# A four-layer graph network on one core: the general path as one loop at the end, norms and neighbour weights in pieces, norm rows by small transfers, transposes beside a product

## The chip, the core and the metric

The kernel runs on one core of a Trainium2 chip. A core has five engines with a queue of instructions each: TensorE (PE; its weight loads are listed apart as PEld), VectorE (DVE), ScalarE (ACT), GpSimd (POOL) and SyncE (SP), which here only issues DMA transfers. GpSimd issues some transfers too. An engine works through its own queue in order; where an instruction needs another engine's result it waits, and all behind it in that queue waits as well. The metric is device microseconds of one execution. The kernel before takes 11451.39 us, the median of three runs (11443.48 to 11453.73).

## What is computed

There are N = 3327 nodes with D = 128 features and a dense matrix adj of zeros and ones, N by N. Four layers follow each other, each behind a layer norm with a relu, and each added to x:

```python
def reference(x, adj, ...):
    relu_norm = lambda x: jnp.maximum(_layernorm(x), 0.0)
    h = relu_norm(x)                                    # layer 0
    x1 = swish(adj @ h @ W + b)
    x = x + swish(adj @ x1 @ W + b)
    h = relu_norm(x)                                    # layer 1: 128 heads of 8
    a = softmax(q @ k.T * 128**-0.5 + adj + adj)        # per head, N x N
    x = x + (a @ v, all heads) @ Wo.T
    h = relu_norm(x)                                    # layer 2
    msg = relu(adj @ h @ W_msg.T + b_msg)
    x = x + gru_cell(msg, h)                            # r, z, n; three products each
    h = relu_norm(x)                                    # layer 3
    d = 1 / sqrt(adj.sum(-1))
    z = leaky_relu(d * (adj @ (d * h)) @ W1 + b1, 0.1)
    d2 = max(|z_i|^2 + |z_j|^2 - 2 z_i . z_j, 0)
    S = exp(-sqrt(d2 + 1e-10) / 2), kept for the 4 largest of a row
    A2 = S + adj;  e = 1 / sqrt(A2.sum(-1))
    return x + e * (A2 @ (e * h)) @ W2 + b2
```

## The kernel before

*Layout.* Nodes lie in T = 26 tiles of P = 128 partitions: partition p holds the rows p*26 + t, one for each tile t. x (`xs`), h and the like are arrays of 128 x 26 x 128 in fp32; a transposed array (`hT`, `zT`, `agg`) has the features on partitions and the nodes along the row. `quads()` gives tiles by fours (six of four and one of two); the norm works in three pieces of 4, 9 and 13 tiles (`CUTS`).

*Order.* The instructions of each engine stand in the order of the program, with a planner that moves them a little within a stage; waits come from the use of tiles and of their memory. A memory pool (`tc.tile_pool`) gives its memory back at its end, and the next pool that takes it waits for the last use. Layer 0 and the attention of layer 1 (an order written out by hand) end at 10565.82 us and are not touched. Everything after them is, and it is called the tail here. In the order of time:

- *Projection* (lines 650 to 669). For each tile SyncE loads o (128 x 9 x 128) from the scratch tensor `ot`; VectorE takes the reciprocal of the sums (658) and multiplies (659); TensorE transposes eight times (664), ScalarE copies (665), TensorE multiplies with Wo (668), and VectorE adds the result to xs (669).
- *Norm of layer 2* (`layernorm_relu`, 146 to 153), after all 26 tiles, in three pieces, each followed by `split` (202 to 205): half of h as a sum of three bf16 arrays, `parts`.
- *Product 2* (`adj_matmul_parts`, 214 to 217): 26 tiles of `adj16`, twice the adjacency in bf16, are loaded (a16, four buffers) and each multiplied with three parts in seven column blocks. `evacuate` copies the seven accumulators to `agg` (177, 179). Behind every such product stands a loop `For_i(0, n_once)` (227) with an fp32 product. `n_once` is read once from a flag that the kernel computes, at line 554, and is 0 for these inputs: the loop is passed without a turn. A further such loop (557) stands between the attention and the projection, with a general attention in it.
- *Gates* (684 to 707): h is transposed to hT (`transposed`, 240 to 244), then per 512 nodes the message, the gates and yT; yT is transposed back and added to xs (711, 712).
- *Norm of layer 3*, times d1 (723), split, and *product 3*.
- *z and squares* (734 to 769): z per quad, leaky relu over all rows (738), transposes to zT, z squared and its sums nsq, z2T = 2 zT; then per 512 nodes zT squared (757), its sum over the features by a matmul (759), and three bf16 rows of it in `n_rows`, on partitions 0, 32 and 64 (765 to 769).
- *Top four* (782 to 788): per tile of 128 nodes TensorE makes 2 z.z of it with all nodes and adds the norm rows (782, 785), ScalarE adds nsq and writes `dist` (786), VectorE finds the eight largest and their indices (MAX8 787, FIND_INDEX8 788).
- *Weights* (791 to 804), after all tiles: near, sim, deg2, d2, y = h*d2 with its split, y stored to `yd` in memory (803), b2 added to xs.
- *Product 4 with gathers* (815 to 830): after the loads of each tile of the product, `beside(t)` lets GpSimd gather the four neighbours' rows of yd by indirect DMA (815), VectorE weigh and add them to a tile g (822, 824), and, LAG = 10 tiles later, TensorE transpose g (829). g has LAG + 2 = 12 buffers. Then the empty loop, the last transposes, the product with W2 (846, 847), scaling (849), the sum with xs (850) and the stores (853).

Of the kernel before, what the change touches and what calls it, by code (L numbers as in the profile page):

```python
# [8 lines left out]
F32 = mybir.dt.float32  # L9
# [11 lines left out]
P = 128  # L21
# [32 lines left out]
def kernel(  # L54
# [79 lines left out]
    def pieces():  # L134
        return [(slice(t0, t1), t1 - t0) for t0, t1 in zip(CUTS, CUTS[1:]) if t1 > t0]

    def layernorm_relu(pool, then=None, tmp=None):
# [7 lines left out]
        for p, n in pieces():  # L145
            nc.vector.tensor_reduce(mean[:, p], xs[:, p], AX.X, ALU.add)
            nc.vector.tensor_scalar_mul(mean[:, p], mean[:, p], 1.0 / D)
            nc.vector.tensor_sub(xc[:, p], xs[:, p], over_t(mean, p.start, n))
            nc.scalar.activation(sq[:, p], xc[:, p], AF.Square)
            nc.vector.tensor_reduce(var[:, p], sq[:, p], AX.X, ALU.add)  # L150
            nc.scalar.activation(rstd[:, p], var[:, p], AF.Sqrt, bias=eps_c, scale=1.0 / D)
            nc.vector.reciprocal(rstd[:, p], rstd[:, p])
            nc.vector.scalar_tensor_tensor(h[:, p], xc[:, p], 0.0, over_t(rstd, p.start, n), op0=ALU.max, op1=ALU.mult)  # L153
            if then is not None:
                then(h, p, n)
        return h
# [42 lines left out]
    def split(pool, parts, y, p, n):  # L199

        rest = pool.tile([P, T, D], F32, name="rest")
        nc.scalar.activation(parts[0][:, p], y[:, p], AF.Copy, scale=0.5)
        nc.vector.scalar_tensor_tensor(rest[:, p], y[:, p], 0.5, parts[0][:, p], op0=ALU.mult, op1=ALU.subtract)
        nc.scalar.copy(parts[1][:, p], rest[:, p])
        nc.vector.tensor_sub(parts[2][:, p], rest[:, p], parts[1][:, p])

    def adj_matmul_parts(agg, parts, lhs, n_once, on_tile=None):
# [19 lines left out]
        with tc.For_i(0, n_once, 1):  # L227
            adj_matmul(agg, lhs, bufs=1)
# [18 lines left out]


# [14 lines left out]
    with tc.tile_pool(name="l0", bufs=1) as pool:  # L263
        h = layernorm_relu(pool)
# [47 lines left out]
        nc.vector.tensor_add(deg[:, T - 1 : T], deg[:, T - 1 : T], fix)  # L312

# [49 lines left out]
    with tc.tile_pool(name="l1", bufs=1) as pool, tc.tile_pool(name="l1_ps", bufs=3, space=PSUM) as ps:  # L363
# [9 lines left out]
        with tc.tile_pool(name="l1_ln", bufs=1) as ln, tc.tile_pool(name="l1_tp", bufs=2, space=PSUM) as tps:  # L373
            hT = transposed(pool, tps, layernorm_relu(ln), "hT")
# [177 lines left out]


# [78 lines left out]

    weights = ctx.enter_context(tc.tile_pool(name="weights", bufs=1))
    w1_s = load_w(w1, [D, D], "w1_s")
    w2_s = load_w(w2, [D, D], "w2_s")
    w_msg_s = load_w(w_msg, [D, D], "w_msg_s")
    w_ih_s = load_w(w_ih, [D, 3, D], "w_ih_s")
    w_hh_s = load_w(w_hh, [D, 3, D], "w_hh_s")
    b_msg_s = load_w(b_msg, [D, 1], "b_msg_s")
    b_ih_s = load_w(b_ih, [D, 3], "b_ih_s")  # L640
    b_hh_s = load_w(b_hh, [D, 3], "b_hh_s")
    b1_s = load_w(dram(b1, 0, [[0, P], [1, D]]), [P, D], "b1_s")
    b2_s = load_w(dram(b2, 0, [[0, P], [1, D]]), [P, D], "b2_s")
    b_rz = weights.tile([D, 3], F32, name="b_rz")
    nc.vector.tensor_add(b_rz, b_ih_s, b_hh_s)


    with tc.tile_pool(name="lo", bufs=3) as pool, tc.tile_pool(name="lo_ps", bufs=2, space=PSUM) as ps:
        wo_s = pool.tile([NH, E, D], F32, name="wo_s", bufs=1)
        nc.gpsimd.dma_start(wo_s, wo)  # L650
        for t in range(T):
            kp = rows_of(t)
            o = pool.tile([P, EA, NH], F32, name="o")
            src = ot.rearrange("e (p t c) -> t p e c", t=T, c=NH)[t]
            for p0, p1 in ((0, kp),) if kp == P else ((0, 112), (112, kp)):
                nc.sync.dma_start(o[p0:p1], src[p0:p1])
            inv = pool.tile([P, NH], F32, name="inv")
            nc.vector.reciprocal(inv[:kp], o[:kp, E, :])
            nc.vector.tensor_mul(o[:kp, :E, :], o[:kp, :E, :], inv[:kp].unsqueeze(1).to_broadcast([kp, E, NH]))
            oT = pool.tile([NH, E, P], F32, name="oT")  # L660
            for half in range(2):
                tp = ps.tile([P, 4, P], F32, name="tp")
                for j in range(4):
                    nc.tensor.transpose(tp[:, j, :kp], o[:kp, 4 * half + j, :], ident[:kp, :kp])
                nc.scalar.copy(oT[:, 4 * half : 4 * half + 4, :kp], tp[:, :, :kp])
            yp = ps.tile([P, D], F32, name="yp")
            for e in range(E):
                nc.tensor.matmul(yp[:kp], oT[:, e, :kp], wo_s[:, e, :], start=(e == 0), stop=(e == E - 1))
            nc.vector.tensor_add(xs[:kp, t, :], xs[:kp, t, :], yp[:kp])


    with tc.tile_pool(name="l2", bufs=1) as pool:
        parts = three_parts(pool)
        h = layernorm_relu(pool, lambda h, p, n: split(pool, parts, h, p, n))
        agg = new_agg(pool)
        adj_matmul_parts(agg, parts, h, n_once)
        with tc.tile_pool(name="l2_tp", bufs=2, space=PSUM) as tps:
            hT = transposed(pool, tps, h, "hT")
        yT = pool.tile([P, NP], F32, name="yT")
        with tc.tile_pool(name="l2_w", bufs=2) as wk2, tc.tile_pool(name="l2_ps", bufs=1, space=PSUM) as ps:  # L680
            for c0, w in chunks(NP, 512):
                hc = hT[:, c0 : c0 + w]
                mp = ps.tile([P, 512], F32, name="mp", bufs=2)
                nc.tensor.matmul(mp[:, :w], w_msg_s, agg[:, c0 : c0 + w], start=True, stop=True)
                msg = wk2.tile([P, 512], F32, name="msg")
                nc.scalar.activation(msg[:, :w], mp[:, :w], AF.Relu, bias=b_msg_s)
                gates = []
                for k in range(2):
                    gp = ps.tile([P, 512], F32, name=f"gp{k}")
                    nc.tensor.matmul(gp[:, :w], w_hh_s[:, k, :], hc, start=True, stop=False)  # L690
                    nc.tensor.matmul(gp[:, :w], w_ih_s[:, k, :], msg[:, :w], start=False, stop=True)
                    gate = wk2.tile([P, 512], F32, name=f"gate{k}")
                    nc.scalar.activation(gate[:, :w], gp[:, :w], AF.Sigmoid, bias=b_rz[:, k : k + 1])
                    gates.append(gate)
                r, z = gates
                hn = ps.tile([P, 512], F32, name="hn")
                nc.tensor.matmul(hn[:, :w], w_hh_s[:, 2, :], hc, start=True, stop=True)
                inn = ps.tile([P, 512], F32, name="inn")
                nc.tensor.matmul(inn[:, :w], w_ih_s[:, 2, :], msg[:, :w], start=True, stop=True)
                n = wk2.tile([P, 512], F32, name="n")  # L700
                nc.vector.scalar_tensor_tensor(n[:, :w], hn[:, :w], b_hh_s[:, 2:3], r[:, :w], op0=ALU.add, op1=ALU.mult)
                nc.vector.tensor_add(n[:, :w], n[:, :w], inn[:, :w])
                nc.scalar.activation(n[:, :w], n[:, :w], AF.Tanh, bias=b_ih_s[:, 2:3])
                y = yT[:, c0 : c0 + w]
                nc.vector.tensor_sub(y, hc, n[:, :w])
                nc.vector.tensor_mul(y, y, z[:, :w])
                nc.vector.tensor_add(y, y, n[:, :w])
            for t0, n in quads():
                tp = ps.tile([P, 4, P], F32, name="tp", bufs=2)
                for j in range(n):  # L710
                    nc.tensor.transpose(tp[:, j, :], slots(yT)[:, t0 + j, :], ident)
                nc.vector.tensor_add(xs[:, t0 : t0 + n, :], xs[:, t0 : t0 + n, :], tp[:, :n, :])


    yd = dpool.tile([NP, D], F32, name="yd")
    keep = ctx.enter_context(tc.tile_pool(name="l3_s", bufs=1))
    with tc.tile_pool(name="l3", bufs=1) as pool:
        d1 = inv_sqrt(keep, deg, "d1")
        y = keep.tile([P, T, D], F32, name="y")
        parts = three_parts(keep)  # L720

        def weighted(h, p, n):
            nc.vector.tensor_mul(y[:, p], h[:, p], over_t(d1, p.start, n))
            split(pool, parts, y, p, n)

        h = layernorm_relu(keep, weighted, pool)
        agg = new_agg(pool)
        adj_matmul_parts(agg, parts, y, n_once)
        z = pool.tile([P, T, D], F32, name="ln_xc")
        with tc.tile_pool(name="l3_ps", bufs=2, space=PSUM) as ps:  # L730
            for t0, n in quads():
                zp = ps.tile([P, 4, D], F32, name="zp")
                for j in range(n):
# [162 lines left out]
```

## Time and profile before

| | us |
|---|---|
| median of three runs | 11451.39 |
| profiled execution | 11471.65 |
| its span | 11469.9 |
| attention ends (last copy of o) | 10565.82 |
| first o tile in use; last sum with xs | 10584.39; 10674.16 |
| product 2: first matmul; first copy of its result | 10685.43; 10795.90 |
| first gate matmul | 10814.45 |
| product 3: first matmul; first copy | 10875.99; 10986.75 |
| first MAX8 | 11057.09 |
| last index found | 11245.71 |
| product 4: first matmul; first gather | 11251.25; 11260.56 |

The mean TensorE clock granted over the span is 0.985 of full speed. A row of a timeline gives the start in us, the busy time, the engine, the line, the operation with output and input, the number of instructions, and in brackets how long the engine had been idle before and what released it; "issue" means that the profile shows nothing that it waited for. SPq is SyncE's queue, where transfers are issued. A row of a group gives the count, the busy time with the mean in ns, and the idle time before it. In the rows of tenths the span is cut into 40 slices, 287 us each.

### The profile page before, as it was taken

The page shows a single profiled execution, that of the slowest core. Times are in us where ns is not written, and L with a number is a line of the kernel's source. Part 1 is how long each engine was busy: PE and PEld are TensorE (multiplying, and loading weights), DVE is VectorE, ACT ScalarE, POOL GpSimd, SP SyncE. Part 2 cuts the span into 40 slices and gives each one's busy share as a digit, 9 for nine tenths or more (in the row PEclk, how much of TensorE's full clock was granted, in tenths as well). Part 3 has the DMA queues.
Part 4 walks back from the last instruction along what each step waited for, and adds up shares of the span by engine and source line. Part 5 has one row for each costly group of instructions (what it writes and reads, how often), then busy time and mean ns, then how long its engine had stood idle before and what let it go on. Part 6 is the DMA issues. An engine that isn't in the chain of part 4 may idle for free. (4 is left out here: it accounts for less than half of the span.)

```text
span 11469.9 us, 212317 instructions
## 1 busy us (share of the span) xinstructions
PE 11060.2 (96%) x80114; PEld 3113.4 (27%) x80114; DVE 9433.5 (82%) x15530; ACT 10214.1 (89%) x9169; POOL 5699.5 (50%) x6205
## 2 busy tenths in 40 slices
PE   9789999999999999999999999999999999999887
PEld 4322222222222222222222222222222222222553
DVE  8578888888888888888888888888888888887464
ACT  0389999999999999999999999999999999998221
POOL 0145555555555555555555555555555555554003
PEclk9899999999999999999999999999999999999998
DMA  7854444343434444444444444434444434343313
GB/s 268 237 118 63 67 64 67 61 69 62 69 61 67 62 69 62 68 62 66 64 66 65 61 67 61 69 60 67 61 68 62 65 57 60 56 61 73 123 57 114
DMA packets 475718, 888.18 MB, mean 77 GB/s; under 512 B 91380, under 2 KB 422629, under 8 KB 439092
## 3 DMA queue, kind: packets, MB, share of 16 engines
q1 hardware_dynamic: 470226, 864.60, 42.6%
q8 instruction: 640, 10.49, 0.4%
q0 software_dynamic: 4448, 9.79, 0.3%
q14 instruction: 404, 3.31, 0.1%
HBM read 763.28 MB, written 110.74 MB: 76 GB/s over the span
## 5 line engine op out<-in xcount | busy, mean ns | idle before, releaser
L484 DVE TENSOR_TENSOR p<-early,a 128x476 f32<-128x476 f32 (+1 forms) x14560 | 8434.5, 644 | 1393.2 <-PE early L479 1160.2
L489 ACT ACTIVATE p<-p 128x2380 f32<-128x2380 f32 (+1 forms) x2912 | 6830.1, 2345 | 8.5
L496 PE MATMUL acc<-p,v 128*9 128x476 f32 (+1 forms) x46592 | 5847.5, 564 | 25.9 <-POOL p L487 7.1
L487 POOL TENSOR_TENSOR p<-p,e 128x476 f32<-128x476 f32 (+1 forms) x2912 | 3535.7, 1214 | 3317.7 <-ACT p L485 3271.5
L485 ACT ACTIVATE p<-late 128x476 f32<-128x476 f32 (+1 forms) x5824 | 4592.2, 923 | 32.3 <-DMA k_in<-kt 21.3
L479 PE MATMUL early<-q,k 32*128 32x476 f32 (+1 forms) x14560 | 2885.5, 477 | 19.9 <-DVE p L484 19.9
L479 PE MATMUL late<-q,k 32*128 32x476 f32 (+1 forms) x8736 | 2797.3, 478 | 64.3 <-ACT p L485 36.2
L360 POOL CAST k<-k_in 128x256 fp32r<-128x256 f32 x2912 | 1943.9, 701 | 1115.9 <-DMA q<-qt 579.2
L479 PEld LDWEIGHTS late<-q,k 32*128 32x128 f32 x8736 | 1065.4, 181 | 4775.4 <-ACT p L485 3318.4
L482 PE MATMUL late<-a,two_i 128*128 128x476 bf16 (+1 forms) x5824 | 2180.8, 374 | 0.0
L479 PEld LDWEIGHTS early<-q,k 32*128 32x128 f32 x14560 | 1147.3, 181 | 26.8 <-DVE p L484 20.6
L496 PEld LDWEIGHTS acc<-p,v 128*9 128x9 f32 x46592 | 709.0, 88 | 1367.8 <-issue 1184.9
L482 PEld LDWEIGHTS <-two_i 128*128 128x128 bf16 x5824 | 556.4, 96 | 1326.6 <-issue 1326.6
L217 PE MATMUL agg_ps<-a,part 128*128 128x512 bf16 (+1 forms) x1638 | 351.7, 375 | 91.7 <-issue 50.1
L177 ACT COPY agg<-agg_ps 128x512 f32<-128x512 f32 x15 | 8.2, 591 | 481.9 <-PE agg_ps L191 290.5
L815 POOL DMA_INDIRECT row<-yd,idx x104 | 99.6, 958 | 461.1 <-DMA yd<-y 393.7
L217 PEld LDWEIGHTS <-part 128*128 128x128 bf16 x1638 | 163.1, 100 | 276.2 <-issue 76.3
L260 POOL TENSOR_SCALAR a<-a_in 128x476 bf16<-128x476 f32 (+2 forms) x156 | 222.5, 1426 | 0.5
L786 ACT ACTIVATE dist<-sp,nsq 128x2048 f32<-128x2048 f32 (+1 forms) x52 | 85.6, 1647 | 114.3 <-PE sp L785 104.0
L394 ACT ACTIVATE qk_st<-pp 128x1024 fp32r<-128x1024 f32 (+1 forms) x52 | 53.2, 1023 | 147.8 <-DMA qt<-qk_st 61.3
L260 POOL TENSOR_SCALAR a<-a 128x476 bf16<-128x476 f32 (+1 forms) x26 | 36.4, 1399 | 295.8 <-DMA a<-in_adjT_dram 295.8
L191 PE MATMUL agg_ps<-a,h 128*128 128x512 f32 (+2 forms) x364 | 148.1, 570 | 24.0 <-DVE h L153 24.0
(186 smaller groups left out, 2602.0 us busy)
## 6 DMA issues: line engine op xcount, KB each, us to landing
k_in<-kt SPq DMA_DIRECT2D x1792, 208.0 KB
v<-vd SPq DMA_DIRECT2D x896, 117.0 KB
a<-in_adjT_dram SPq DMA_DIRECT2D x50, 1663.5 KB
a<-adj SPq DMA_DIRECT2D x78, 831.8 KB
q<-qt SPq DMA_DIRECT2D x3072, 14.9 KB
a_in<-in_adjT_dram SPq DMA_DIRECT2D x125, 238.0 KB
qt<-qk_st SPq DMA_DIRECT2D x25, 1024.0 KB
kt<-qk_st SPq DMA_DIRECT2D x25, 1024.0 KB
```

The source lines that it names most:

```text
L191: nc.tensor.matmul(acc[c][:, :w], lhs[:kp, t, :], a[:kp, c0 : c0 + w], start=(t == 0), stop=(t == T - 1))
L217: nc.tensor.matmul(acc[c][:, :w], part[:, t, :], a[:, c0 : c0 + w], start=(t == 0 and i == 0), stop=(t == T - 1 and i == 2),)
L260: nc.gpsimd.tensor_scalar(a2[:kp, :w], a, 2.0, None, op0=ALU.mult)
L360: nc.gpsimd.tensor_copy(k, slots(k_in)[:, t : t + 2, :])
L479: nc.tensor.matmul(sp[:, :we], pairs[t // 2][r, t % 2, :], q4[r, :we], start=True, stop=ways[i] != "I")
L482: nc.tensor.matmul(late[:, i - n_d, :we], two_i, a2[:, :we], start=False, stop=True)
L484: nc.vector.tensor_tensor(p8[:, places[i], :we], early[i][:, :we], a2[:, :we], op=ALU.add)
L485: nc.scalar.activation(p8[:, places[n_d] : places[3] + 1, :we], late[:, :, :we], AF.Exp)
L487: nc.gpsimd.tensor_tensor(p8[:, places[3], :we], p8[:, places[3], :we], e_a[:, :we], op=ALU.mult)
L489: nc.scalar.activation(p8[:, :5, :we], p8[:, :5, :we], AF.Exp)
L496: nc.tensor.matmul(acc[32 * i : 32 * i + EA, :w], v4[:kp, i, t, :], p8[:kp, PLACES[t % 2][i], :w], start=(t == 0), stop=(t == T - 1),)
L815: nc.gpsimd.indirect_dma_start(out=row, out_offset=None, in_=yd, in_offset=bass.IndirectOffsetOnAxis(ap=idx[:, t, k : k + 1], axis=0),)
```

## The change

- *The general path in one place.* The tail becomes a function `tail(general)`. It is called with False first; at the end of the kernel stands one loop `For_i(0, n_once)`, which holds the general attention, the reload of xs from a copy `x1d` that is stored after layer 0, and `tail(True)`. The loops behind the products and the one before the projection are gone, and the flag is read at the end.
- *Norms in pieces as rows come.* `layernorm_relu` returns h and a function `done(t)`; a piece is worked off as soon as its rows are added to xs: in the projection's loop, and in the loop over the quads that adds the GRU's result. `split` takes y already halved, as `halved` and `d1_half` make it.
- *Transposes beside product 2.* A quad of h is transposed at each odd tile of the product; the stage of transposes in front of the gates is gone.
- *z and squares by quads.* The leaky relu, z squared (on GpSimd now), its sums, zT and z2T (both straight from the transposes in PSUM, on ScalarE) come quad by quad. The norm rows are no longer summed by a matmul: nsq (128 x 26) is split into three bf16 arrays, each stored to a scratch row of `nd` by a small transfer, and one more transfer reads the three rows as `n_rows`, on three partitions.
- *Neighbour weights in pieces.* `second(p, n)` does lines 791 to 803 for a piece of tiles as soon as the top-four loop has passed it; y and its split are GpSimd's work for the first two pieces and VectorE's for the last; yd is stored in three pieces. The indices get a min with the last row. The sum with b2 goes to GpSimd, after product 3.
- *Buffers.* LAG is 6 and g has 8 buffers. The pools are merged to a single one for layers 2 and 3 (`l23`), whose arrays take each other's names and memory: `zT` that of hT, `z2T` that of yT, `gT` that of ln_sq. The pool `lo` lies inside it.

Lines that only move are left out of this diff:

```diff
-    def adj_matmul_parts(agg, parts, lhs, n_once, on_tile=None):
+    def adj_matmul_parts(agg, parts, on_tile=None):
...
             evacuate(agg, acc)
-        with tc.For_i(0, n_once, 1):
-            adj_matmul(agg, lhs, bufs=1)
...
+    def in_pieces(f):
+        todo = [slice(t0, t1) for t0, t1 in zip(CUTS, CUTS[1:]) if t1 > t0]
+        def done(t):
+            while todo and todo[0].stop <= t:
+                p = todo.pop(0)
+                f(p, p.stop - p.start)
+        return done
...
+        nc.gpsimd.dma_start(x1d, xs)
...
                 for t in range(T):
...
                     nc.vector.tensor_add(xs[:kp, t, :], xs[:kp, t, :], yp[:kp])
+                    done(t + 1)
...
+                def transpose_quad(t):
+                    if t % 2 and left:
+                        t0, n = left.pop(0)
+                        tp = tps.tile([P, 4, P], F32, name="tp")
+                        for j in range(n):
+                            nc.tensor.transpose(tp[:, j, :], h[:, t0 + j, :], ident)
+                        nc.vector.tensor_copy(slots(hT)[:, t0 : t0 + n, :], tp[:, :n, :])
+                adj_product(agg, y, parts, transpose_quad)
...
-            nc.vector.scalar_tensor_tensor(z, z, 0.1, z, op0=ALU.mult, op1=ALU.max)
-            zT = transposed(pool, ps, z, "zT")
-        nc.vector.tensor_mul(zz, z, z)
-        nc.vector.tensor_reduce(nsq, zz, AX.X, ALU.add, negate=True)
-        nc.scalar.activation(z2T, zT, AF.Copy, scale=2.0)
+                    nc.vector.scalar_tensor_tensor(z[:, q], z[:, q], 0.1, z[:, q], op0=ALU.mult, op1=ALU.max)
+                    for j in range(n):
+                        nc.tensor.transpose(tp[:, j, :], z[:, t0 + j, :], ident)
+                    nc.scalar.activation(slots(z2T)[:, q, :], tp[:, :n, :], AF.Copy, scale=2.0)
+                    nc.scalar.copy(slots(zT)[:, q, :], tp[:, :n, :])
+                    nc.gpsimd.tensor_mul(zz[:, q], z[:, q], z[:, q])
+                    nc.vector.tensor_reduce(nsq[:, q], zz[:, q], AX.X, ALU.add, negate=True)
-                nc.tensor.matmul(np_[:, :w], neg_ones[:, :PR], zzT[:, :w], start=True, stop=True)
...
+            for i in range(3):
+                nc.vector.tensor_copy(n3[:, i, :], src)
+                if i < 2:
+                    nc.vector.tensor_sub(rest[:, i, :], src, n3[:, i, :])
+                    src = rest[:, i, :]
+                nc.sync.dma_start(nd[i].rearrange("(p t) -> p t", t=T), n3[:, i, :])
+            nc.sync.dma_start(n_rows, nd)
...
+            def second(p, n):
+                nc.vector.tensor_scalar(idx[:, p, :4], idx[:, p, :4], NP - 1, None, op0=ALU.min)
+                nc.vector.tensor_scalar(near[:, p], top[:, p, :4], 0.0, None, op0=ALU.min)
+                nc.scalar.activation(sim[:, p], near[:, p], AF.Sqrt, bias=tiny_c, scale=-1.0)
+                nc.scalar.activation(sim[:, p], sim[:, p], AF.Exp, scale=-0.5)
...
+                engine = nc.gpsimd if p.stop < T else nc.vector
+                engine.tensor_mul(y[:, p], h[:, p], over_t(d2_half, p.start, n))
+                split_unless_general(pool, parts, y, p, engine)
+                nc.sync.dma_start(yd.rearrange("(p t) f -> p t f", t=T)[:, p], y[:, p])
...
                 nc.vector.max_index(idx[:, t, :], top[:, t, :], dist)
+                done(t + 1)
...
-        gs, LAG = [], 10
+            gs, LAG = [], 6
...
+    tail(False)
     n_once = nc.values_load(n_gen[0:1, 0:1], min_val=0, max_val=1)
     with tc.For_i(0, n_once, 1):
...
+        nc.sync.dma_start(xs, x1d)
+        tail(True)
```

## Prediction

> **What bounds the kernel now.** I read the page first, then the trace in the order of time.
>
> ```profile
> span 11469.9 us, 212317 instructions
> PE   9789999999999999999999999999999999999887
> L217 PE MATMUL agg_ps<-a,part 128*128 128x512 bf16 (+1 forms) x1638 | 351.7, 375 | 91.7 <-issue 50.1
> L815 POOL DMA_INDIRECT row<-yd,idx x104 | 99.6, 958 | 461.1 <-DMA yd<-y 393.7
> ```
>
> TensorE is busy in 96% of the span, but only the last three digits of its row, which drop to 8 and 7, are touched: up to the end of the attention (10565.8 us) all engines but POOL get the same instructions in the same order, and POOL has one more, the store of x1d. It stands ahead of three weight loads that are issued at 359 us and first used at 378.8; its 1.7 MB cost some 4.3 us at 400 GB/s, which that slack hides. So the prediction is about 904 us, 10566 to 11470. The timelines of TensorE, VectorE and SyncE cut them at the points where an engine waited:
>
> ```profile
> 10584.39 0.95 DVE L658 RECIPROCAL inv<-o 128x128 f32<-128x128 f32 x1 [17.92 <-DMA o<-ot]
> 10674.16 0.29 DVE L669 TENSOR_TENSOR xs<-xs,yp 127x128 f32<-127x128 f32 x1 [2.91 <-PE yp L668]
> 10685.43 24.78 PE L217 MATMUL agg_ps<-a,part 128*128 128x512 bf16 x113 [11.31 <-ACT part L202]
> 10795.90 2.21 DVE L179 COPY agg<-agg_ps 128x512 f32<-128x512 f32 x4 [95.36 <-PE agg_ps L217]
> 10814.45 1.10 PE L684 MATMUL mp<-agg,w_msg_s 128*128 128x512 f32 x2 [0.82 <-DVE hT L244]
> 10857.35 6.31 PE L711 MATMUL tp<-ident,yT 128*128 128x128 f32 x26 [3.37 <-DVE yT L707]
> 10875.99 34.36 PE L217 MATMUL agg_ps<-a,part 128*128 128x512 bf16 x159 [12.32 <-ACT part L202]
> 10986.75 2.21 DVE L179 COPY agg<-agg_ps 128x512 f32<-128x512 f32 x4 [88.98 <-PE agg_ps L217]
> 10993.42 12.02 PE L734 MATMUL zp<-w_s,agg 128*128 128x128 f32 x52 [5.52 <-issue]
> 11057.09 3.63 DVE L787 MAX8 top<-dist 128x8 f32<-128x3327 f32 x1 [8.52 <-ACT dist L786]
> 11245.71 0.19 DVE L791 TENSOR_SCALAR near<-top 128x104 f32<-128x104 f32 x1
> 11254.23 0.32 SPq L803 DMA_DIRECT2D yd<-y  x1
> 11260.56 1.10 POOL L815 DMA_INDIRECT row<-yd,idx  x1 [393.73 <-DMA yd<-y]
> 11285.75 0.38 PE L217 MATMUL agg_ps<-a,part 128*128 128x512 bf16 x1 [2.42 <-issue]
> 11339.63 10.65 PE L217 MATMUL agg_ps<-a,part 128*128 128x512 bf16 x40 [0.81 <-issue]
> 11357.36 0.94 POOL L815 DMA_INDIRECT row<-yd,idx  x1 [26.07 <-DVE g L822]
> 11440.34 0.47 PE L829 MATMUL tp<-ident,g 128*128 128x128 f32 x1 [5.21 <-issue]
> ```
>
> Two stretches, of the squares and of the last product, in the view by windows (us, then busy time and instructions of PE, PEld, DVE, ACT, POOL, then PEclk, DMA share, GB/s):
>
> ```profile
> 11000.00:11050.00 50.00, 26.52 (x70) 13.77 (x70) 40.81 (x66) 10.37 (x11) 0.00 (x0) 0.64 0.00 0
> 11300.00:11350.00 50.00, 19.63 (x57) 6.29 (x57) 6.43 (x19) 0.00 (x0) 23.67 (x26) 0.55 0.28 90
> ```
>
> The reader is to see the bracket: how long the engine had been idle and for whom. Most stages begin with such a gap, and the change goes at these gaps. Inside, the bound changes: the loads and TensorE in the output projection, TensorE in the products, VectorE in the squares (10993 to 11057) and in the top four (188.6 us, 7.25 a tile, 99% busy), and in the last product GpSimd's gathers: 104 of them about 1.25 apart.
>
> **The change, stage by stage**
>
> 1. *Projection start.* Before, an empty loop (L557) stands between attention and projection: last copy at 10565.8, first load issued at 10578.75, data 5.6 later. Without it the loads go out as soon as the ot stores are through: data at about 10569.5, so 15 earlier. The stage took 89.8, of which 83.7 is its steady 26 x 3.22; its first five tiles waited for loads while four a16 loads (3.4 MB, 8.5 us at 400 GB/s) ran among them. Now a16 reuses this stage's memory and comes after it: I keep 2.5 of the excess. The norms of tiles 0 to 12 now lie in VectorE's queue between tiles: 12.9 us of its work (by the like rows of the later norms), against a slack of 0.75 a tile (inv, mul and add take 2.47 of 3.22), behind which inv, mul and the xs add of the next tile wait, then TensorE. Half fits in; 6 stays. End 10569.5 + 83.7 + 2.5 + 6 = 10661.7 instead of 10674.5: **12** gained (6 to 16).
>
> 2. *Product 2 starts.* TensorE waited 11.3 for norm and split (L202). Now piece 0 has long been ready, but a16[0] is late next: it waits for the stage's last use of the memory. One load, issued with its fellows, lands about 4.8 after issue (the four loads before: issue 1.6 before the first byte, 8.5 for all). Gain 11.3 - 4.8 = **6.5** (4 to 8).
>
> 3. *Product 2 to gates.* From the first accumulator copy to the first gate matmul it was 18.5: copies (2.2), the loop (8.1), transposes of h in a stage of their own (8.2). The last two go but for some 1.4 of start: 14.9. The 26 transposes now sit beside the product at 0.16 each: -4.2. **10.7** (8 to 12). TensorE has no cover here, so they count in full.
>
> 4. *Gates to product 3.* Gates unchanged (43). The 18.6 from the first transpose to the product shrink, as piece 0's norm starts after its own quad; piece 1 then holds TensorE about 1.2. **4** (2 to 6).
>
> 5. *Squares and norms.* 70.3 from evacuation to the first MAX8. Gone: the loop (4.5); the zz pass over all rows; norm rows per 512 columns on VectorE, which was busy 40.8 of 50 us at 11000 to 11050. Now per quad VectorE has two products, a leaky max and a reduction, 2.75 us by the like rows; 6.5 quads are 18; zz on GpSimd (1.3 each by L487's 1214 ns for 476) and PSUM copies on ACT lie beside. VectorE is through at about 11012.5, and as from L782 to MAX8 before (11.3), MAX8 comes at about 11024: **33** (27 to 37). Against it: norm rows now go by four small transfers in two hops through memory, for which this trace has no like. The Trainium skill, "DMA: Bandwidth & Descriptors", section "Anatomy of one DMA", gives every transfer some 2 us that no size removes. Added up as four, that is 8 and the stage gains 25; three run side by side, so two hops, 4 to 6, and seven z matmuls (about 0.8 each at the clock of 0.64 here) stand ahead of the first matmul that needs the rows. I take the cover as whole; without it, 5 less.
>
> 6. *Top four.* Pieces 0 and 1 put seven small operations each (1.2 us) between MAX8s: **-2.5**. Four more table loads go to ACT. The trace has 1.28 us for one; "ScalarE: Activation LUTs", section "What ACT_TABLE_LOAD costs", says 2.66 with the drain. On the path they would cost 5.1 or 10.6. But the order has a MAX8 of 3.63 between the piece's near and the sum that waits for sqrt, load and exp: 1.95 by the trace, 3.3 by the page. Both fit; I charge nothing. GpSimd is otherwise idle and takes the y and splits of these pieces.
>
> 7. *End.* From the last index (E = 11245.7) 224.2 to the end. The product still starts at E + 5.5, since its a16 tiles take dist's memory and wait for the last index. Only piece 2 of yd is left, half the bytes but behind three a16 loads: gathers start at about E + 11.3 instead of E + 14.85. Before, 130 of gathers took 167: 37 of pauses. From 11283 to 11339.6 TensorE issues a matmul each 2.8 us with nothing shown that it waits for (the "issue" line), while gathers run back to back; then all 12 g tiles are full and GpSimd waits 26. With 8 tiles and a lag of 6, g frees at the same product tile (two behind the gather), but the first burst is about 10 tiles rather than 12: TensorE recovers earlier, and I put pauses at 20 (0 to 37, the ends being no crawl and the same crawl). After the gathers: loop (5.3) gone, seven transposes instead of eight to ten one by one; 25.7 to the last store; then register load and the one loop at the end, 6 by the loops here (4.5 to 8.1). 11.3 + 130 + 20 + 25.7 + 6 = 193, or 195 with the copies of the accumulators behind a late product: **29** (5 to 50).
>
> Sum 12 + 6.5 + 10.7 + 4 + 33 - 2.5 + 29 = 92.7. The profiled execution took 11471.65, so it would take 11379. It is 20 above the median 11451.39; some of that could be the crawl being worse under the profiler, so of the expected 17 less in pauses I carry only some over to the median: 11451.4 - 92 = **11359**.
>
> **Rivals**
> - *The pauses stay* (a new wait for the old one): TensorE crawls whenever gathers run, its start has not moved, and 8 tiles fill sooner. For it: the coupling at two tiles behind is the same. Gain 92 - 25 = 67: 11384.
> - *The crawl goes nearly*: transposes break the burst. Pauses 0 to 5: 11340. Against it: GpSimd's rate is not changed, and a second, short crawl (11389 to 11400) came without full g tiles.
> - *Slower*: one mechanism, TensorE beside the gathers. It now has to keep g tiles turning with two thirds of the buffers; if every fill restarts a crawl of 57, the gathers of 26 tiles in bursts of 8 meet three instead of one. Each costs 40 to 50 of delay; it decides from 92 more than now, that is with both extra crawls whole. For it only the unknown cause; against it the second burst of 14 tiles before, which cost 11.
> - *The norm pieces in the projection fill no slack* and a16 starts cold: stages 1 and 2 give 0 to 5 instead of 18.5: 11374.
>
> **How the numbers follow.** My sum 0.5; pauses stay 0.2; crawl goes 0.13; projection slower 0.12; slower kernel 0.05. Ends of the gather term (+21, -24) and of stages 1 and 5 (about 7 each) give 11320 to 11407, holding all but the last case and the tails. Its own range is 11340 to 11378. Under 0.2% (23 us), which is what can be told from no change, lies little: only half of several gains failing at once would come there. Faster 0.93, same 0.03, slower 0.04.
>
> **What would show it.** The first inv within 5 us of the last attention copy; xs adds still 3.2 apart but with a lump after tiles 4 and 13; product 2 led by a wait for a16, not for part; first gate matmul 3 us after the copies; MAX8 33 sooner, counted from zp's evacuation; the top-four loop longer by under 4; a shorter wait than 26 in GpSimd's gathers; a last loop of about 6. It is wrong if MAX8 waits for n_rows, if the projection's period rises above 3.4, or if TensorE's one-by-one stretch covers more of the last product than before.

## The result: 54 us less, where 92 were forecast

The changed kernel takes 11392.72 us (median of five, 11381.04 to 11394.47), the kernel before beside it 11446.42: a ratio of 0.9949, 95% interval 0.9934 to 0.9963. The interval leaves out no change, and the time is inside the forecast range of 11320 to 11407, but the gain is 54 us instead of 92. Two later jobs ran the changed kernel again beside the kernel before: 74 and 81 us less there (tables below).

The profiled execution of the changed kernel, 11392.72 us like the median, has a span 79 us shorter than the one shown before. Of its page:

```profile
span 11391.0 us, 212068 instructions
PE   9789999999999999999999999999999999999998
```

The starts of its stages, in the timelines of VectorE, TensorE and GpSimd:

```profile
10592.27 0.65 DVE L520 COPY o<-acc 105x471 f32<-105x471 f32 x1 [4.61 <-PE acc L511]
10596.55 0.95 DVE L620 RECIPROCAL inv<-o 128x128 f32<-128x128 f32 x1 [3.63 <-DMA o<-ot]
10686.85 0.29 DVE L631 TENSOR_TENSOR xs<-xs,yp 127x128 f32<-127x128 f32 x1 [2.91 <-PE yp L630]
10691.22 27.12 PE L228 MATMUL agg_ps<-a,part 128*128 128x512 bf16 x126 [0.43 <-DMA a<-adj]
10805.72 1.10 PE L657 MATMUL mp<-agg,w_msg_s 128*128 128x512 f32 x2 [1.17 <-ACT agg L187]
10848.61 3.71 PE L696 MATMUL tp<-ident,yT 128*128 128x128 f32 x16 [3.37 <-DVE yT L680]
10861.45 23.73 PE L228 MATMUL agg_ps<-a,part 128*128 128x512 bf16 x107 [4.40 <-ACT part L213]
10972.06 2.22 DVE L189 COPY agg<-agg_ps 128x512 f32<-128x512 f32 x4 [83.02 <-PE agg_ps L228]
11010.23 3.63 DVE L779 MAX8 top<-dist 128x8 f32<-128x3327 f32 x1 [12.83 <-ACT dist L778]
11214.76 0.19 DVE L752 TENSOR_SCALAR near<-top 128x52 f32<-128x52 f32 x1
11226.67 2.23 POOL L791 DMA_INDIRECT row<-yd,idx  x1 [88.25 <-ACT part L215]
```

TensorE's row ends in 9, 9, 8 where it ended in 8, 8, 7. The three brackets that were 11 to 18 us are now 0.4 to 4.4; VectorE's before the first MAX8 has grown from 8.5 to 12.8. Differences of neighbouring rows, set against the same rows of before:

| step | before | after | gain | forecast |
|---|---|---|---|---|
| 1 attention's last copy to the last sum with xs | 108.3 | 94.6 | 13.8 | 12 |
| 2 to product 2 | 11.3 | 4.4 | 6.9 | 6.5 |
| 3 to the first gate matmul | 129.0 | 114.5 | 14.5 | 10.7 |
| gates | 42.9 | 42.9 | 0 | 0 |
| 4 first transpose of yT to product 3 | 18.6 | 12.8 | 5.8 | 4 |
| product 3, to its first copy | 110.8 | 110.6 | 0.2 | 0 |
| 5 to the first MAX8 | 70.3 | 38.2 | 32.2 | 33 |
| 6 top four, to near | 188.6 | 204.5 | -15.9 | -2.5 |
| 7 to the end | 224.2 | 176.2 | 48.0 | 29 |
| all of the tail | 904.1 | 798.7 | 105.4 | 92.7 |

Three things stand out. The top four became slower by 16 us. The end gained more than forecast in this execution: GpSimd's 104 gathers took 131 us from first to last instead of 167, with no pause. In the profile of before, TensorE had for a while issued one matmul in 2.8 us beside the gathers; this is called the crawl below, and here it is absent. And the attention, whose instructions are the same, ended 26.5 us later (10592.27 against 10565.82), which is why 105 in the tail are 79 in the span. The other 25 of the 79 are not in the medians at all, since the profiled execution of before was 25 slower than its median.

### The profile page after: what moved, and what is told of

The parts are those of the page before. It is cut to its first block, busy times and chain, and to the rows that moved or that the text cites. A ratio compares the mean times of both kernels' runs of the same rounds, so it can differ in the third digit from the quotient of the medians.

```text
span 11391.0 us, 212068 instructions
## 1 busy us (share of the span) xinstructions
PE 11065.1 (97%) x80100; PEld 3098.6 (27%) x80100; DVE 9408.1 (83%) x15508; ACT 10238.7 (90%) x9182; POOL 5727.5 (50%) x6218
## 5 line engine op out<-in xcount | busy, mean ns | idle before, releaser
L504 ACT ACTIVATE p<-p 128x2380 f32<-128x2380 f32 (+1 forms) x2912 | 6757.4, 2321 | 14.2 <-DVE p L499 0.5
L500 ACT ACTIVATE p<-late 128x476 f32<-128x476 f32 (+1 forms) x5824 | 4529.2, 897 | 38.9 <-DMA vd<-v_st 20.3
L228 PEld LDWEIGHTS <-part 128*128 128x128 bf16 x1638 | 161.7, 99 | 188.6 <-DVE d_half L759 13.7
L774 PE MATMUL sp<-yT,hT 128*128 128x512 f32 (+1 forms) x364 | 168.2, 603 | 3.6 <-ACT hT L726 2.1
```

What stands on the lines that cost most here:

```text
L228: nc.tensor.matmul(acc[c][:, :w], part[:, t, :], a[:, c0 : c0 + w], start=(t == 0 and i == 0), stop=(t == T - 1 and i == 2),)
L500: nc.scalar.activation(p8[:, places[n_d] : places[3] + 1, :we], late[:, :, :we], AF.Exp)
L504: nc.scalar.activation(p8[:, :5, :we], p8[:, :5, :we], AF.Exp)
L774: nc.tensor.matmul(sp[:, c0 : c0 + w], slots(zT)[:, t, :], z2T[:, cols], start=True, stop=False)
```

## The experiments

The tail and its two doubtful stages are read from each kernel's own trace; "attention" is the time from its first to its last copy of o, and "top four" that from the first MAX8 to the last index. The kernel before of each job is the yardstick for the times. Job 1 held before_again, rows_65, copy_last and before_with_copy (kernel before 11480.84), job 2 after_again, before_no_loops, lag_10 and norm_late (11482.48), job 3 the rest (11498.09).

| kernel | median us | to before of its job | attention | tail | top four | gathers |
|---|---|---|---|---|---|---|
| before_again | 11484.44 | (one run) | 9881.4 | 908.5 | 188.7 | 165.8 |
| after_again | 11408.61 | -74, 0.9937 (0.9923 to 0.9951) | 9881.2 | 833.4 | 204.7 | 153.6 |
| after_c | 11417.04 | -81, 0.9930 (0.9917 to 0.9944) | 9897.1 | 835.6 | 204.7 | 154.3 |
| rows_65 | 11409.35 | -71, 0.9938 (0.9925 to 0.9952) | 9887.4 | 820.1 | 192.6 | 156.1 |
| rows_65_b | 11406.74 | -91, 0.9921 (0.9907 to 0.9934) | 9895.2 | 816.4 | 192.4 | 154.1 |
| copy_last | 11421.30 | -60, 0.9946 (0.9933 to 0.9960) | 9887.9 | 837.1 | 204.6 | 154.8 |
| before_with_copy | 11496.85 | +16, 1.0012 (1.0004 to 1.0019) | 9883.8 | 906.9 | 188.7 | 167.6 |
| before_no_loops | 11455.22 | -27, 0.9976 (0.9967 to 0.9985) | 9878.1 | 882.4 | 188.7 | 166.8 |
| lag_10 | 11427.57 | -55, 0.9951 (0.9937 to 0.9965) | 9882.6 | 851.6 | 204.5 | 168.6 |
| norm_late | 11406.42 | -76, 0.9937 (0.9924 to 0.9951) | 9874.9 | 829.8 | 204.5 | 157.4 |
| g_26 | 11474.55 | -24, 0.9976 (0.9967 to 0.9986) | 9900.2 | 882.7 | 192.4 | 131.1 |
| short_burst | 11392.77 | -105, 0.9911 (0.9897 to 0.9925) | 9896.8 | 811.0 | 192.4 | 153.2 |

### Was the yardstick's profile an odd one? The kernel before, again

No edit.

> The kernel before, unchanged, once more. My theory: the stretch in which TensorE issued a matmul each 2.8 us beside the gathers, and the 26 us wait of GpSimd behind it, belonged to that one profiled execution (11471.65) and not to the ordinary ones (11446). Then the 104 gathers take some 131 us from first to last instead of 167, and the end of the attention is reached not at 10566 but at 10575 to 10592. Rival: the crawl is in every execution; then gathers take about 167 again and the attention ends at 10566.

Gathers took 165.8 and TensorE crawled as in the first page: my theory fell, and the rival held for the crawl. The attention ended at 10574, eight later than in the first page. Here the crawl is in an execution of 11484 where the median of the kernel before is 11481; so in this job it is an ordinary part of the time, not an accident of one page.

### Three norm rows on 65 partitions

```diff
-            n_rows = pool.tile([3, NP], BF16, name="n_rows")
-            one_rows = pool.tile([3, P], BF16, name="one_rows")
+            n_rows = pool.tile([65, NP], BF16, name="n_rows")
+            one_rows = pool.tile([65, P], BF16, name="one_rows")
             nc.vector.memset(one_rows, 1.0)
+            nc.gpsimd.memset(n_rows, 0.0)
...
-            nc.sync.dma_start(n_rows, nd)
+            for i in range(3):
+                nc.sync.dma_start(n_rows[32 * i : 32 * i + 1], nd[i : i + 1])
```

> The changed kernel with the three norm rows back on partitions 0, 32 and 64 of a zeroed tile of 65 (as before the change), filled by three row transfers in place of one. Theory 1: TensorE loses time at each change between a matmul over 128 rows and one over 3, because the weights of the one are no longer loaded under the other; then the top-four loop is 7.2 to 7.3 us a tile again instead of 7.82, VectorE waits for nothing in it, and the kernel is 12 to 15 us faster than the changed one (about 11379). Rival: TensorE is slowed by where z2T and zT now lie (they took the names of yT and hT); then the period stays 7.8 and the time 11393.

> Three norm rows on 65 partitions once more, beside the changed kernel. In the profile of its first run the top four took 12 us less; its five times did not show it against the changed kernel of another job. Theory 1 says 10 to 14 us below the changed kernel of this job; if what is gained in the top four is lost again in the last product, the two are within 4.

> The changed kernel a third time, to stand beside the next three. On the chip of the last two jobs: 11400 to 11420, top four 204.6, gathers 153 to 156.

The cause shows in the trace of the changed kernel. Its groups in a window inside the top four (11030 to 11190), here the rows of VectorE and TensorE:

```profile
L774 PE MATMUL sp<-yT,hT 128*128 128x512 f32 x245 | 120.9, 629 | 0.0
L779 DVE MAX8 top<-dist 128x8 f32<-128x3327 f32 x21 | 76.2, 3626 | 9.0 <-ACT dist L778 9.0
L777 PEld LDWEIGHTS <-one_rows 3*128 3x128 bf16 x147 | 10.4, 92 | 26.1 <-issue 18.4
```

and the same groups of the kernel before (11070 to 11230):

```profile
L787 DVE MAX8 top<-dist 128x8 f32<-128x3327 f32 x22 | 79.3, 3606 | 0.0
L782 PE MATMUL sp<-z2T,zT 128*128 128x512 f32 x272 | 126.8, 602 | 0.0
L785 PEld LDWEIGHTS <-one_rows 65*128 65x128 bf16 x156 | 15.3, 98 | 21.1 <-issue 7.6
```

VectorE did not wait before and waits 9.0 us in 21 tiles now, for a dist that TensorE makes late; TensorE's fp32 matmul of the same shape went from 602 to 629 ns in the mean. How it loses time is seen in the timelines of the weight loads (PEld) and matmuls of the changed kernel, one above the other:

```profile
11112.22 3.09 PEld L774 LDWEIGHTS sp<-yT,hT 128*128 128x128 f32 x8 [0.32 <-issue]
11115.96 0.54 PEld L777 LDWEIGHTS <-one_rows 3*128 3x128 bf16 x4 [0.65 <-issue]
...
11112.22 3.81 PE L774 MATMUL sp<-yT,hT 128*128 128x512 f32 x8
11115.97 1.03 PE L777 MATMUL sp<-n_rows,one_rows 3*128 3x512 bf16 x4
```

and of rows_65_b:

```profile
11103.15 0.10 PEld L779 LDWEIGHTS <-one_rows 65*128 65x128 bf16 x1
11103.58 0.53 PEld L779 LDWEIGHTS <-one_rows 65*128 65x128 bf16 x3 [0.33 <-issue]
11104.23 2.24 PEld L776 LDWEIGHTS sp<-yT,hT 128*128 128x128 f32 x6
...
11103.58 1.03 PE L779 MATMUL sp<-n_rows,one_rows 65*128 65x512 bf16 x4
```

With 65 rows the first weights are loaded 0.43 us ahead of their matmul, under the last fp32 one (11103.15 against 11103.58). With 3 rows they are loaded only as it starts (11115.96 and 11115.97). The same happens on the way back: with 3 rows the fp32 weights at 11112.22 come with their matmul, with 65 they are loaded at 11104.23, 0.21 us ahead of theirs at 11104.44. There are four such changes in a tile, and it takes 7.82 us (11199.67 to 11207.49 between MAX8s) where VectorE needs 7.25. With 65 rows the top four are 192.4 to 192.6, 12 less. The placement of zT and z2T was the same in both, so that rival is out. The times agree within each job: in the first, rows_65 was 12.0 below copy_last, the changed kernel with three rows and only x1d placed otherwise (next section); in the third, rows_65_b was 10.3 below after_c, both in medians of five whose ranges overlap. Against the changed kernel of another job it can't be seen. The Trainium skill, "TensorEngine Tiling (Array Packing)", "Key Properties", says that a change of the tiling mode drains TensorE. The weight loads that no longer overlap agree; the trace shows the overlap lost, not the name of the mode.

### The 26 us of the attention: the copy x1d

```diff
     adj16 = dpool.tile([T, P, N], BF16, name="adj16")
+    x1d = dpool.tile([P, T, D], F32, name="x1d")
+    nc.gpsimd.dma_start(x1d, xs)
```

(and both lines taken out where the change put them).

> The changed kernel with x1d allocated after kt, qt, vd, ot and adj16 in memory instead of ahead of them (its store at the same point). Theory 2a: the attention's loads run slower because x1d moved these tensors by 1.7 MB; then the attention ends 20 to 28 us earlier than in the changed kernel's profile (at 10565 to 10572) and the time is about 11366. Rival 2b: the end of the attention varies between executions or chips, whatever the tail; then it ends where the other kernels of this job end it, and the time stays 11385 to 11398.

The second run is the kernel before with x1d where the change has it:

> The kernel before with x1d alone: allocated ahead of kt and stored after layer 0, never read. Theory 2a: the attention is 20 to 28 us longer than that of the kernel before in this job, and the kernel slower by as much (11466 to 11474 against 11446). Rival 2b: no difference that can be told (11440 to 11452).

copy_last's attention is 9887.9 beside 9887.4 of rows_65 in the same job: the placement does nothing. Over all traces the same instructions of the attention took 9870.8 to 9900.2 us; the two pages at first compared, 9870.8 and 9898.9, happen to be near the ends of that. Within one job they lie 5 to 8 us apart, in the first two with kernels before and after the change among each other. So most of the 26.5 is variation between executions and chips. before_with_copy is slower in its times by 16 us, with an interval that excludes no difference, while its trace has 2.4 more in the attention than before_again and 1.6 less in the tail. This fits neither forecast. A part of 16 may be the price of the copy; this is left open.

### Does the crawl go with the change?

> The changed kernel, unchanged, once more. Theory 3: whether TensorE crawls beside the gathers goes with the chip or the execution, and not with the change; on a chip where the kernel before crawls, the changed one does too: 104 gathers in 150 to 157 us instead of 131.5, tail 820 to 840 us, time 20 to 30 below a kernel before of 11480 plus its gain, some 11415 to 11425. Rival: the change in its own form (unlike its two variants of the last job) ends the crawl; then gathers take 131 and the tail 799.

Yes, it crawls here too: gathers 153.6, tail 833; only the time, 11408.61, is below the 11415 forecast. In its window from 11230 to 11260 TensorE did 11 matmuls beside 25 gathers; in the first profile of the same kernel, from 11250 to 11300, 256 beside 41 (columns as in the prediction; the last three are the granted clock, the DMA share and GB/s):

```profile
11230.00:11260.00 30.00, 5.79 (x11) 1.14 (x11) 6.69 (x20) 0.00 (x0) 22.69 (x25) 0.55 0.29 81
```

```profile
11250.00:11300.00 50.00, 50.00 (x256) 25.07 (x255) 12.68 (x40) 3.19 (x12) 37.81 (x41) 1.00 0.75 250
```

The gathers keep the same pace, one per 1.25 us, so they alone don't force the crawl. The granted clock falls to 0.55 with it, but TensorE is busy for only 5.79 of the 30 us, so a slow clock doesn't make the crawl. The crawl was in the first trace of the kernel before and in every trace of the later three jobs, which ran on three chips, and not in the first one of the changed kernel. From the last index to the end, before_again needs 227.9 and after_again 210.7: 17 us, where 29 were forecast.

### The lag of 10 again, and more g tiles

```diff
-            gs, LAG = [], 6
+            gs, LAG = [], 10
```

> The changed kernel with a lag of 10 and 12 g tiles as before. My step: 12 tiles let the first burst of gathers run longer, TensorE crawls longer, pauses are 10 to 17 us more than in the changed kernel on this chip (gathers 165 instead of 155; time +10 to +15). Rival: the coupling is at two product tiles behind in both, and the time is the same within 5.

Gathers 168.6, 15 more than after_again; the time 19 more. The step held, a little stronger than forecast. GpSimd's timeline, first pauses of lag_10 and of after_again:

```profile
11308.80 0.95 POOL L791 DMA_INDIRECT row<-yd,idx  x1 [29.37 <-DVE g L798]
```

```profile
11273.52 0.94 POOL L791 DMA_INDIRECT row<-yd,idx  x1 [10.89 <-DVE g L798]
```

The first burst ran 71 us there and 51 here: 14 tiles and 10, that is the g tiles and two more in the row buffers. The next takes the limit away (the edit is on rows_65_b):

```diff
-                g = gpool.tile([P, D], F32, name="g", bufs=LAG + 2)
+                g = gpool.tile([P, D], F32, name="g", bufs=T)
```

> As the last, with 26 g tiles instead of 8, so that GpSimd never waits for TensorE. Theory 4: TensorE crawls for as long as gathers go out back to back; then it crawls from 17 us after the first gather to the last gather, gathers take 131 to 134, and TensorE has 17 to 20 tiles still to do: 75 to 85 us more of product after the gathers; the kernel is 30 to 60 us slower than the one with 8. Rival: the crawl is a thing of some 30 to 60 us of its own that ends by itself; then gathers take 131, the product ends near them, and the kernel is 15 to 25 us faster.

The window view of g_26 inside the gathers, and after them:

```profile
11250.00:11300.00 50.00, 10.09 (x18) 1.88 (x18) 13.31 (x40) 0.00 (x0) 37.76 (x40) 0.50 0.26 70
11360.00:11410.00 50.00, 47.19 (x225) 23.01 (x226) 0.00 (x0) 2.92 (x11) 0.00 (x0) 0.91 0.56 186
```

GpSimd never waits, gathers take 131.1, and TensorE crawls for as long: 18 matmuls in 50 us, then 225. The crawl comes late at both ends: it begins some 20 us after the first gather (11216.2) and ends at 11363.2, 16 after the last (11347.3). 131 us lie between the last gather and the end, 98 of them of the product where 75 to 85 were forecast, and the kernel is 68 slower than with 8 tiles, where 30 to 60 were forecast. So where the crawl occurs, the pause of GpSimd is no loss to be removed: it is what lets TensorE run. The trace speaks against one other cause, a wait for instructions. In the 50 us shown of the first profile TensorE took 511 instructions (256 matmuls, 255 weight loads), and the queue q8 moved two transfers of the kind "instruction"; in g_26, from 11240 to 11360, it moved none. So no transfer of that kind was under way there that TensorE could have waited for. The last run goes the other way:

```diff
-            gs, LAG = [], 6
+            gs, LAG = [], 3
...
-            with tc.tile_pool(name="l3_g", bufs=8) as gpool, tc.tile_pool(name="l3_gps", bufs=1, space=PSUM) as g_ps:
+            with tc.tile_pool(name="l3_g", bufs=4) as gpool, tc.tile_pool(name="l3_gps", bufs=1, space=PSUM) as g_ps:
```

> As rows_65_b, with a lag of 3, 5 g tiles and 4 row buffers instead of 6, 8 and 8. By theory 4 the first burst of gathers ends after some 8 tiles instead of 10, so the first crawl is about 10 us shorter and the gathers take 140 to 150: 5 to 15 us faster than rows_65_b. Rival: every stop of the gathers costs as much as it saves: the same within 4, or slower since rows now wait for their buffers.

14 us faster than rows_65_b and 24 faster than after_c in the same job: 0.9911 of the kernel before, the best of all here. But not, as forecast, by shorter gathers: they took 153.2 (154.1). The first long pause still came after 40 gathers; it was 5.0 us instead of 12.0, but more short ones followed. TensorE's first crawl did get shorter: 11260 to 11267 us, after a wait of 11.8 for the copy of a transposed tile, where that of rows_65_b ran from 11227 to 11260. What fell is the time from the last gather to the end, 42.9 to 37.8, since TensorE was less behind when they ended. The traces give 5 of the 14; the rest is not located.

### The loops, and the order of the norm pieces

before_no_loops leaves out the general path with its four loops and the reading of the flag:

```diff
-        with tc.For_i(0, n_once, 1):
-            adj_matmul(agg, lhs, bufs=1)
...
-    n_once = nc.values_load(n_gen[0:1, 0:1], min_val=0, max_val=1)
-    with tc.For_i(0, n_once, 1):
...
```

> The kernel before without the four loops that are passed without a turn and without the reading of the flag; the general path is left out. By my terms the loops cost 7.8 (before the projection), 8.1, 4.5 and 5.3 us; with what stands idle around them 28 to 38 less than the kernel before. If the first loop alone hid the latency of the loads of the attention's results, only 15 to 20 less.

27 less, one below the forecast's lower end of 28. By stage against before_again: first data 8.6 earlier, of which 3.9 are given back as the projection's loop gets longer (94.5 against 90.6, a16 loads still among its own); product 2 to gates 9.0; to MAX8 3.8; the end 8.5. TensorE's timeline of before_again has a loop's gap, and behind it slow transposes; without the loop eight take 1.06 instead of 1.97, at a granted clock of 1.00 (10800 to 10803) instead of 0.50 (10814 to 10818):

```profile
10814.64 1.97 PE L240 MATMUL tp<-ident,h 128*128 128x128 f32 x8 [9.13 <-issue]
```

```profile
10800.39 1.06 PE L238 MATMUL tp<-ident,h 128*128 128x128 f32 x8 [1.21 <-DVE agg L179]
```

So the loops are about a third of the gain. The wait for the norm before product 2 did not go with them (11.3 still).

The last of these runs moves the norm pieces of the changed kernel behind the projection's loop:

```diff
                     nc.vector.tensor_add(xs[:kp, t, :], xs[:kp, t, :], yp[:kp])
-                    done(t + 1)
+                done(T)
```

> The changed kernel with all three norm pieces of layer 2 behind the projection instead of in its loop. By my steps: the projection's loop is 3 to 6 us shorter, but TensorE then waits about 11 us for the norm as before instead of 4.4, so 2 to 5 us slower in all than the changed kernel. If the pieces cost nothing in the loop: 6.5 to 7 slower.

No difference (11406.42 and 11408.61), but not for either reason given: in its trace the first piece's mean is still formed inside the projection (by VectorE at 10591.88, 69 us before the loop's last sum). Here the planner put that piece where its rows were there, though the program names it later. What this run doesn't tell is the worth of the pieces.

## Why the prediction was right in sign and range, and where it failed

*Steps 1 to 5 held*, together 73 us against 66 forecast. The first o tile is in use 14.3 earlier (15 said). I charged 6 for norm pieces that find no slack and kept 2.5 for loads: the projection took 90.3 against 92.2 forecast, so the two together cost 6.6 instead of 8.5. (The figures of step 1 make 12.8, not the 12 that it states.) Product 2 starts after 4.4 us (4.8), led by the wait for a16, with two quads of transposes in that time. Step 3 was 3.8 too cautious. In step 5, the transfers of the norm rows were covered: the last norm part is ready at 10997.2, the matmul that needs the rows follows the seven z matmuls at 11005.9 without a wait, 8.7 later. The gain of 25 that followed from adding the fixed cost of four transfers (the Trainium skill, "DMA: Bandwidth & Descriptors", "Anatomy of one DMA") did not come true: the chain was hidden. Besides, that section is about transfers that GpSimd issues, not about every transfer as the prediction says, and these four are SyncE's. Here the first of the three stores is issued at 10996.56 and the transfer that reads the rows at 11000.60, 4.0 us later.

*Step 6 failed.* It said: "Pieces 0 and 1 put seven small operations each (1.2 us) between MAX8s: -2.5." That much is nearly right (192.4 with 65 rows against 188.7 leaves 3.7). The table loads cost nothing that shows: in the profile of the changed kernel the load takes 1.28 us and exp starts 1.32 after the end of sqrt (11113.86 to 11115.18), so the 2.66 that the prediction quotes is not seen. But it took the loop as bound by VectorE, with TensorE unchanged. In the kernel before, TensorE's own period there was 7.11 us against VectorE's 7.25, a slack of 0.14, and in the window from 11100 to 11150 it was as busy as VectorE (50.00 and 49.76 of 50 us). I had read the second number alone. Two rows of TensorE's timeline of the kernel before, one tile apart:

```profile
11101.76 1.03 PE L785 MATMUL sp<-n_rows,one_rows 65*128 65x512 bf16 x4
11108.87 1.03 PE L785 MATMUL sp<-n_rows,one_rows 65*128 65x512 bf16 x4
```

A matmul over 3 rows in place of 65 has the same time by itself (378 and 379 ns); what costs is the change between it and the fp32 one, which took TensorE's period from 7.11 to 7.82. Missing: 12 to 13 us.

*Step 7 was too large*: 17 on a chip with the crawl instead of 29, though the pauses came as put: 153.6 is 130 and 23 (20 forecast). After the last gather 45.3 remained, where I had 25.7 and 6, because TensorE was still behind with the product (its last matmul ended 11.5 after the last gather). I had written that as a case ("behind a late product") with 2 us; it is 14.

*The mechanism of the slower rival is real, its point was not reached.* TensorE beside gathers can cost 68 us (g_26), but fewer buffers make it better, not worse: the forecast of three crawls for 8 tiles had the sign of the dependence wrong.

*The copy x1d* was put at nothing; the 16 us of before_with_copy leave open whether that is so.

*What was luck.* The time is inside the outer range but outside the 11340 to 11378 that my sum was given for itself. It lies near the 11384 of the case in which the pauses stay, yet the pauses shrank as forecast; steps 6 and 7 took the gain away. And in the first pair of profiles the tail's 105 comes near 92.7 because steps 6 and 7 were missed by 13 and 19 in opposite directions.

In the later jobs the two errors make 13 and 12, against 7 gained in steps 1 to 5: 92.7 becomes 75, which is what the tails of before_again and after_again differ by (908.5 and 833.4), and near what two of three jobs measured (74, 81). The 54 of the first is lower still, though the intervals of the three ratios overlap, so noise alone could make them differ. The kernel before was 34 to 52 us faster there than in the later jobs, and the changed kernel's trace from there has no crawl. If the kernel before had none there either, it had no pauses to shorten. That is argued and not shown: there is no trace of those five executions, and the one on record beside three of them, with the crawl, took 11471.65, 18 more than the slowest.

## What to carry to other kernels

A small matmul that shares a loop with full ones must be judged by what it does to their weight loads, not by its own time: here 65 rows, 62 of them zeros, were 12 us cheaper in the loop than 3. Where two engines are within a few per cent of each other in a loop, a change that is free on the one that sets the pace still has to be checked on the other. And before taking a wait away, ask what it protects: here more buffers for the gathers cost 68 us.

## What was not expected of the hardware

While gathers go out one per 1.25 us, TensorE on three chips issues a matmul only each 2.8 us and waits for nothing that the trace shows. A matmul of 512 columns then takes 0.58 us at a granted clock of 0.50 (g_26), against 0.38 otherwise, which is a small part of the 2.8. The crawl lasts about as long as the gathers do, 16 to 20 us behind them (g_26), and is absent in one trace with the same gathers and the same instructions. What starts it is open. The same attention code took 9870.8 to 9900.2 us, a spread of 0.3%, about half the measured effect of the whole change: here two profiles could not be set against each other end to end, only stage by stage.
